# A transformer block on one core: where x + gate * bias is added, and when the MLP's rows are normed

## The chip, the cores and the metric

The kernel runs on one core of a Trainium2 chip. The metric is device time in microseconds (us) for one execution, as the median of several runs. One execution was also recorded by the hardware profiler. From that record come the profile (a page of summaries) and the trace behind it, which can be asked for waits, groups of instructions, stretches of time and a timeline. The engines are called by the profile's short names where a line is quoted: PE is TensorE's matmul, PEld its weight load, DVE is VectorE, ACT ScalarE, POOL GpSimd and SP SyncE, whose queue issues transfers.

## The reference

A conditioned transformer block (adaptive layer norm) in float32: batch B = 2, N = 2048 tokens, C = 576 features, 16 heads of 36, MLP width 2304.

```python
mod = silu(c) @ w_ada + b_ada
sh_msa, sc_msa, g_msa, sh_mlp, sc_mlp, g_mlp = split(mod, 6)
xn = _ln(x, 1e-6) * (1 + sc_msa) + sh_msa
q, k, v = heads(xn @ w_qkv + b_qkv)
q, k = _ln(q, 1e-5, qn_g, qn_b), _ln(k, 1e-5, kn_g, kn_b)
o = softmax(q @ k.T * 36**-0.5) @ v
x = x + g_msa * (o @ w_proj + b_proj)
xn2 = _ln(x, 1e-6) * (1 + sc_mlp) + sh_mlp
h = gelu(xn2 @ w1 + b1)
x = x + g_mlp * (h @ w2 + b2)
```

## The kernel before

The branch that runs is `block_of_small`. Its stages follow one another; each is a Python loop that is fully unrolled.

**Start.** `mod`, the shifts and scales of x, is computed from `w_ada`. Row tiles of 128 tokens are normed on VectorE (`rows_normed`: statistics L271, aggregate L273, root on ScalarE L275, reciprocal L277, scaling L278, and a copy on ScalarE L279), transposed by TensorE into PSUM (`transposed`, L348 and L349) and scaled by ScalarE on their way out (`modulated`, L356).

**For each of two batches: inputs, attention, outputs.** `inputs` makes q, k and v of 16 token tiles (matmuls L370 and L381). `attend` runs 8 pairs of heads (p) by 4 query blocks of 512 (qb) by 4 groups of keys (g): 128 steps a batch. A step computes scores (L981), their exponentials on ScalarE (L985) and the product with the values of the step before (L994); VectorE adds that product to the tile `ot` (copied by L1040 for g = 0, added by L1042 after). Eight PSUM banks go round: a step takes eight for scores and one for the sums. When a query block is finished (`finish`), its sums of exponentials go to DRAM and back, spread over partitions (`den`, L1009 and L1010 on SP's queue). The function `divided` comes steps later: a reciprocal (L1013), a product (L1014) and five transfers to `qo` on SP's queue (L1019). What comes later is kept in a list of lists, `later`: `later[3]` is run three steps on. `take_q` and `take_k` fetch the next block's queries (SP's queue) and the next pair's keys (GpSimd's queue, L764 and L767); the small operations that split their last rows (L777, L778) are put into `later` as well. `hooks` holds functions that are called at a step (p, qb, g).

`outputs` projects the 16 token tiles (L370 and L381 again). For tile t, `residual(t)` loads x by GpSimd's queue (L1071) into a scratch tile, `biased(t)` adds gate * bias on GpSimd (L1075), `evicted` multiplies the PSUM tile by the gate on VectorE (L1080), and `summed` adds the two on VectorE (L1087) and stores the row tile in `x1_dram` (L1088). In the first batch the scratch tiles are pieces of `kr`, which held the keys; in the second they are a pool of twelve. In the second batch `outputs` also runs, between its tiles, the first MLP block's loads, norms and transposes, and five sums of w1's parts on VectorE (`weight_sums`, L1244 to L1248), whose operands `wr` and `wb` SP's queue loads.

**First MLP product.** It is done by a scheme with seven products instead of eight (m = 1 to 7) over 8 blocks of 512 tokens; each block has 9 jobs, and two jobs make one pass of the loop. `whole_part` (L1320) multiplies m = 2, 4, 5, 6, 7, 3, 1; `halved_part` (L1334) adds the last 64 features; `gelu_stored` copies the m = 1 sum out of PSUM on ScalarE (L1346), combines the products on VectorE (L1347 to L1354) in the tile `cs`, applies gelu (L1358) and stores. Four sums of tokens in the tiles `ss` (`token_sums`, L1291 to L1294) are needed before m = 5, 6 and 3. `ahead(job)` prepares the next block: its `at(offset)` names the token tile whose base job lies `offset` jobs back. A tile is loaded one job ahead of its base job (L823, GpSimd's queue, three tiles in turn), normed in it, transposed in the job after it (L1379, then L1385 on ScalarE) and its last chunk in the second job after. Bases are jobs 0, 2, 4 and 6 of each block. Nine being odd, they fall on the first job of a pass in even blocks and on the second in odd ones. Five sums of w2's parts on VectorE (`later_sums`, L1397) stand at the ends of some passes.

**Second MLP product** (`second_product`, L1470), which the change leaves alone.

**Order.** TensorE's instructions are in program order throughout, VectorE's in inputs, in attention and from the second batch's outputs on. The other engines' orders come from a planner that works with estimated times. Waits are put in by the framework, from the regions that instructions read and write; a tile in a new pool waits for the users of the tiles that had its place.

Of the kernel before, what the change touches and what calls it, by code (L numbers as in the profile page):

```python
# [8 lines left out]
F32 = mybir.dt.float32  # L9
# [3 lines left out]
ALU = mybir.AluOpType  # L13
# [3 lines left out]
P = 128  # L17
# [14 lines left out]
def dit_block(  # L32
# [309 lines left out]

    def transposed(src, tail):

        ps = s_tile()
        t4, t1 = ps[:, 0, :], ps[:, 1, :]
        for k in range(FULL):
            nc.tensor.transpose(t4[:, k * P : (k + 1) * P], src[:, k * P : (k + 1) * P], ident)  # L348
        nc.tensor.transpose(t1[:, :P], tail, ident)  # L349
        return t4, t1  # L350

    def modulated(dst, src, which, b):

        t4, t1 = transposed(*src)
        for k in range(NKC):
            nc.scalar.activation(  # L356
                dst[:, k, :],
                t4[:, k * P : (k + 1) * P] if k < FULL else t1[:, :P],
                AF.Identity,
                bias=mod[:, which, k, b : b + 1],  # L360
                scale=mod[:, which + 1, k, b : b + 1],
            )
# [353 lines left out]
    def block_of_small():  # L716
# [114 lines left out]

        def input_by_feature(b, rows):
            xnt = xs["pool"].tile([P, NKC, P], F32, name="xnt", bufs=2)
            modulated(xnt, rows, 0, b)
            return xnt
# [127 lines left out]
        def attend(b, pool, hooks):  # L963
# [65 lines left out]
            for p, qb, g in [*steps, (None, None, None)]:  # L1029
# [5 lines left out]
                if behind is not None:  # L1035
                    bp, bqb, bg, bpts = behind
                    acc = values(bp, bpts)
                    if bg == 0:
                        ot = pool.tile([P, BLK], F32, name="ot", bufs=2)
                        nc.vector.tensor_copy(ot, acc)  # L1040
                    else:
                        nc.vector.tensor_tensor(ot, acc, ot, ALU.add)  # L1042
                    if bg == NG - 1:
                        later[3].append(finish(bp, bqb, ot))
                if (p, qb, g) in hooks:
# [8 lines left out]
        def output_weights(b):  # L1054
            pool, close = opened("wp", side="right")
            wp = pool.tile([P, FULL, C], F32, name="wp")
            wp4 = pool.tile([P, 1, HALF], F32, name="wp4")
            nc.sync.dma_start(out=wp, in_=w_proj[0:512, :].rearrange("(k p) f -> p k f", p=P))
            last_chunk(wp4, w_proj, 1, HALF)
            return (wp, wp4, gate_rows(pool, 0, b), gate_rows(pool, 1, b), pool), close  # L1060

        def outputs(b, weights, between, scratch):


            wp, wp4, g1, gb1, pool = weights
            x1s = {}

            def residual(t):
                if t < NT:
                    x1s[t] = scratch[t % len(scratch)]  # L1070
                    nc.gpsimd.dma_start(out=x1s[t], in_=x[b, t * P : (t + 1) * P, :])  # L1071

            def biased(t):
                if t < NT:
                    nc.gpsimd.tensor_tensor(x1s[t], x1s[t], gb1, ALU.add)  # L1075

# [6 lines left out]
            def summed():  # L1083
                while products:
# [4 lines left out]
                    residual(t + 6)  # L1089
                    biased(t + 3)  # L1090

# [5 lines left out]
            for t in range(6):  # L1097
                residual(t)
            for t in range(3):
                biased(t)  # L1100
            for t0 in range(0, NT, 4):
# [27 lines left out]
        close_psum = opened_psum(s=4)  # L1129
        xnt = input_by_feature(0, (x_first[:, :512], x_first[:, 512:]))  # L1130
        loaded = [tile_loaded(x[0, t * P : (t + 1) * P, :], nc.sync) for t in (1, 2)]
        weights, close_weights = input_weights()
        for b in range(B):
# [32 lines left out]
            def output_opened():  # L1166
# [7 lines left out]
                (4, 0, 1): output_opened,  # L1174
            }
            if b == 0:
                hooks |= {
                    (0, 2, 1): ada_opened,
                    (1, 0, 2): ada_gates,
                    (2, 0, 2): ada_feature_rows,  # L1180
                    (2, 0, 3): ada_features,
                }
            with tc.manual_schedule(engines={mybir.EngineType.DVE}):
                attend(b, att, hooks)
# [4 lines left out]
            if b + 1 < B:  # L1189
# [4 lines left out]
                }  # L1194
                outputs(b, wp, between, [kr[:, c, a * 640 : a * 640 + C] for c in range(4) for a in range(3)])
                xnt = opening["xnt"]
# [82 lines left out]
        hidden = [m2.tile([P, NF, PAIR], F32, name="hidden0")]  # L1279
        m1, close_m1 = opened("m1")  # L1280
        ss = {m: m1.tile([P, 2, PAIR], F32, name=f"s{m}") for m in (1, 2, 4)}
        stack = ExitStack()
# [20 lines left out]
        def whole_part(n, f, side, first):  # L1303
# [13 lines left out]
            out_m = sums_of(side)  # L1317
            for m in (2, 4, 5, 6, 7, 3, 1):
                for k in range(2):
# [22 lines left out]
        def gelu_stored(n, f, side):  # L1342
            cs = m1.tile([P, 5, PAIR], F32, name="cs", bufs=2)
            flat = ps_m[side].rearrange("p b c -> p (b c)")
# [16 lines left out]
        def ahead(job):  # L1361
# [7 lines left out]

            if todo := at(-1):  # L1370
                rows_ahead[todo] = mlp_loaded(*todo, nc.gpsimd)
            if todo := at(0):
                rows_ahead[todo] = tile_normed(rows_ahead[todo])
# [34 lines left out]
        rows_ahead = {}  # L1408
        rows_ahead[1, 0] = mlp_loaded(1, 0, nc.gpsimd)
        token_sums(0)  # L1410
# [131 lines left out]
```

## Time and profile before

| What | Value |
|---|---|
| Median of 3 runs (lowest to highest) | 3267.62 us (3267.26 to 3267.93) |
| Profiled execution, own time | 3270.42 us |
| Its span, first to last instruction | 3268.6 us |
| Busy: PE, PEld, DVE, ACT, POOL | 3218.1, 1888.4, 1456.7, 1504.6, 318.0 us |
| First batch: attention from, outputs from, next inputs' end | 269, 1051, 1384 us |
| Second batch: outputs from | 2137 us |
| First MLP product, second MLP product from | 2216, 2771 us |

In a line of the timeline the columns are start, duration, engine, source line, operation, tiles (out<-in), shapes and count; brackets hold the engine's idle time just before, and what ended it. A line of the waits names who waited, the line that released it, the total, the number of times and the longest. "L278" is line 278 of the kernel. The ends of matmul records are modelled and overlap the next start, so losses on TensorE are best counted from start to start.

### The profile page before, as it was taken

Reading aid. Unit: us, or ns where it says so; the run is one execution under the profiler, and the core shown is the slowest. Engines: PE = TensorE matmul, PEld = TensorE weight load, DVE = VectorE, ACT = ScalarE, POOL = GpSimd, SP = SyncE. Lnnn points to the kernel's source line nnn. Section 1 sums busy time; section 2 is a strip of 40 time slices with the busy share of each in tenths; the row PEclk is TensorE's granted clock in tenths of the full one; section 3 lists DMA queues with packets and bytes.
Section 4 is the critical chain, followed back from the end, with each engine's and each line's share of the span. In section 5 each row is a group of like instructions: output and inputs, shape, how many; then the busy total and the mean of one; then the engine's idle time right before and its main releaser. Section 6 shows DMA issues by size and latency. Waiting matters only on the chain.

```text
span 3268.6 us, 46758 instructions
## 1 busy us (share of the span) xinstructions
PE 3218.1 (98%) x18143; PEld 1888.4 (58%) x18143; DVE 1456.7 (45%) x2073; ACT 1504.6 (46%) x2952; POOL 318.0 (10%) x369
## 2 busy tenths in 40 slices
PE   7999999999999999999999999999999999999998
PEld 5775333333334777633333333367888888777776
DVE  4664333333333466533333333364455444454454
ACT  2335666666665033466666666614554552000000
POOL 1111001001100111100000000040000000111111
PEclk9999999999999999999999999999999999999999
DMA  3112312112211411121121211154322222433321
GB/s 129 26 27 64 86 44 69 47 43 56 55 36 30 144 29 24 27 64 36 44 47 42 45 43 35 35 184 150 118 83 81 88 78 97 168 120 119 116 102 38
DMA packets 122803, 234.28 MB, mean 72 GB/s; under 512 B 21891, under 2 KB 64844, under 8 KB 120524
## 3 DMA queue, kind: packets, MB, share of 16 engines
q1 hardware_dynamic: 104244, 182.07, 18.3%
q0 software_dynamic: 17600, 47.64, 5.5%
q8 instruction: 146, 2.39, 0.3%
q10 hardware_dynamic: 728, 1.48, 0.2%
q14 instruction: 85, 0.70, 0.1%
HBM read 125.96 MB, written 56.91 MB: 56 GB/s over the span
## 4 chain that ended last, share of the span: by engine, by line
PE 95%; DMA 1%; issue 1%; DVE 1%; ACT 0%; POOL 0%; SPq 0%; DVEq 0%; POOLq 0%; ACTq 0%
PE b L994 28%; PE b L981 19%; PE s L370 14%; PE s L1470 14%; PE m L1320 12%; PE m L1334 2%; PE s L381 2%; PE one L1320 2%; PE s L884 1%; PE t L1379 1%; DMA wb<-in_w_dram 1%; PE s L348 0%; DMA wq<-in_w_qkv_dram 0%; DVE xt L278 0%; DMA wa<-in_w_ada_dram 0%
## 5 line engine op out<-in xcount | busy, mean ns | idle before, releaser
L985 ACT ACTIVATE pt<-b 128x512 f32<-128x512 f32 x2048 | 1058.0, 610 | 487.2 <-PE b L994 271.1
L994 PE MATMUL b<-pt,vt 128*64 128x512 f32 x4096 | 935.1, 599 | 0.0
L994 PEld LDWEIGHTS b<-pt,vt 128*64 128x64 f32 x4096 | 271.8, 136 | 581.4 <-issue 439.4
L981 PE MATMUL b<-qm,km 32*128 32x512 f32 x4096 | 567.9, 614 | 2.0 <-DVE vt L936 1.6
L1042 DVE TENSOR_TENSOR ot<-b,ot 128x512 f32<-128x512 f32 x192 | 132.7, 691 | 656.2 <-PE b L994 656.2
L981 PE MATMUL b<-qe,ke 16*128 16x512 f32 x2048 | 423.5, 789 | 0.0
L370 PE MATMUL s<-wq,xnt 128*128 128x288 f32 x1536 | 393.3, 411 | 1.1 <-DMA wq<-in_w_qkv_dram 1.1
L1470 PE MATMUL s<-ws,as 128*128 128x288 f32 x1440 | 351.8, 406 | 0.0
L981 PEld LDWEIGHTS b<-qm,km 32*128 32x128 f32 x4096 | 192.4, 185 | 271.8 <-ACT pt L985 206.5
L370 PEld LDWEIGHTS s<-wq,xnt 128*128 128x128 f32 x1536 | 286.8, 191 | 92.9 <-issue 18.5
L1470 PEld LDWEIGHTS s<-ws,as 128*128 128x128 f32 x1440 | 273.7, 190 | 75.5
L1013 DVE RECIPROCAL den<-den 128x512 f32<-128x512 f32 x64 | 213.9, 3342 | 1.8 <-DMA den<-den_dram 1.8
L1320 PE MATMUL m<-s,wb 128*128 128x256 f32 x864 | 210.2, 379 | 4.5 <-DVE s L1294 3.5
L1320 PE MATMUL m<-xnt,wb 128*128 128x256 f32 x864 | 214.5, 384 | 0.0
L1040 DVE COPY ot<-b 128x512 f32<-128x512 f32 x64 | 44.2, 691 | 339.1 <-PE b L994 321.0
L1320 PEld LDWEIGHTS m<-s,wb 128*128 128x128 f32 x864 | 164.1, 190 | 27.5 <-DVE s L1294 3.9
L1320 PEld LDWEIGHTS m<-xnt,wb 128*128 128x128 f32 x864 | 159.6, 191 | 32.9 <-issue 12.6
L981 PEld LDWEIGHTS b<-qe,ke 16*128 16x128 f32 x2048 | 108.8, 184 | 114.1 <-issue 112.8
L1347 DVE TENSOR_TENSOR cs<-m,cs 128x512 f32<-128x512 f32 x72 | 49.7, 691 | 236.6 <-ACT cs L1346 158.6
L1358 ACT ACTIVATE cs<-cs,b_sb 128x512 f32<-128x512 f32 x144 | 103.9, 722 | 88.6 <-DVE cs L1353 88.6
L1470 PE MATMUL s<-ws,hidden 128*128 128x288 f32 x576 | 142.3, 406 | 0.0
L356 ACT ACTIVATE xnt<-s,mod 128x128 f32<-128x128 f32 x180 | 66.6, 458 | 159.8 <-PE s L349 159.8
(160 smaller groups left out, 2572.0 us busy)
## 6 DMA issues: line engine op xcount, KB each, us to landing
gelu<-cs SPq DMA_DIRECT2D x144, 256.0 KB
hidden<-gelu SPq DMA_DIRECT2D x16, 2304.0 KB
den<-den_dram SPq DMA_DIRECT2D x128, 128.0 KB
qm<-qo SPq DMA_DIRECT2D x192, 64.0 KB
xr<-x_dram SPq DMA_DIRECT2D x32, 288.0 KB
out_dram<-y POOLq DMA_DIRECT2D x32, 288.0 KB, 3.7
qe<-qo SPq DMA_DIRECT2D x256, 32.0 KB
qo<-ot SPq DMA_DIRECT2D x104, 72.0 KB
```

The lines of the kernel that those rows point to most:

```text
L356: nc.scalar.activation(dst[:, k, :], t4[:, k * P : (k + 1) * P] if k < FULL else t1[:, :P], AF.Identity, bias=mod[:, which, k, b : b + 1], ...
L370: nc.tensor.matmul(outs[a], stationary(k, a), moving(k, a), start=(first and k == 0), stop=(not first and k == FULL - 1),)
L381: nc.tensor.matmul(outs[a], stationary(FULL, a)[r], moving(FULL, a)[r], start=first, stop=not first)
L981: nc.tensor.matmul(ps, k[r, keys], q[r, :], start=first, stop=not first)
L985: nc.scalar.activation(pt[:, h, :], banks[2 * c + h], AF.Exp, scale=SCALE)
L994: nc.tensor.matmul(acc[64 * h : 64 * h + 64, :], vt[:, v0 : v0 + 64], pt[:, h, :], start=pt is pts[0][0], stop=pt is pts[-1][0],)
L1013: nc.vector.reciprocal(den, den)
L1042: nc.vector.tensor_tensor(ot, acc, ot, ALU.add)
L1320: nc.tensor.matmul(out_m[m], wb[:, slot[m], k, f * P : (f + 1) * P], moving[m](k), start=k == 0 and (m == 1 or (first and m in (2, 5, 6))) ...
L1334: nc.tensor.matmul(out_m[m], w[r, f * P : (f + 1) * P], a[r, FULL, t * PAIR : (t + 1) * PAIR], start=first and m != 4, stop=not first and ...
L1358: nc.scalar.activation(part, part, AF.Gelu, bias=b1_sb[:, g : g + 1])
L1470: nc.tensor.matmul(ms[m], stationary[m][:, f, :], ws[m][:, f, :], start=(f == 0), stop=(f == HF - 1))
```

## The change

- `residual_begun` runs in attention, at hooks (3 + t // 4, t % 4, 3) for t = 0 to 16: GpSimd's queue loads a row tile of x into `spare` (a piece of `kr`), the tile before it gets gate * bias added on GpSimd and is stored in `x1_dram`. For t = 0 it loads the gate row as well. `outputs` then loads from `x1_dram` in place of x, and adds no bias. In attention GpSimd's instructions are in program order.
- In the last pair of heads `divided` is put two steps on, not three.
- In the first MLP product a token tile is normed one job ahead of its base job and loaded three jobs ahead; tile (1, 0) is still normed in job 0, and two tiles are loaded before the loop.
- The `cs` tiles are two fixed ones, allocated ahead of the `ss` tiles. In the first job m = 1 comes third.
- The very first transposes write their last chunk into a second PSUM tile.

```diff
@@ -340,18 +340,18 @@
         nc.vector.tensor_copy(xn[:, C:], xn[:, 512:576])
         return xn[:, :512], xn[:, 512:]
 
-    def transposed(src, tail):
+    def transposed(src, tail, apart=False):
 
         ps = s_tile()
-        t4, t1 = ps[:, 0, :], ps[:, 1, :]
+        t4, t1 = ps[:, 0, :], (s_tile() if apart else ps)[:, 1, :]
         for k in range(FULL):
             nc.tensor.transpose(t4[:, k * P : (k + 1) * P], src[:, k * P : (k + 1) * P], ident)
         nc.tensor.transpose(t1[:, :P], tail, ident)
         return t4, t1
 
-    def modulated(dst, src, which, b):
-
-        t4, t1 = transposed(*src)
+    def modulated(dst, src, which, b, apart=False):
+
+        t4, t1 = transposed(*src, apart)
         for k in range(NKC):
             nc.scalar.activation(
                 dst[:, k, :],
@@ -829,9 +829,9 @@
         def input_rows(b, t, queue):
             return tile_normed(tile_loaded(x[b, t * P : (t + 1) * P, :], queue))
 
-        def input_by_feature(b, rows):
+        def input_by_feature(b, rows, apart=False):
             xnt = xs["pool"].tile([P, NKC, P], F32, name="xnt", bufs=2)
-            modulated(xnt, rows, 0, b)
+            modulated(xnt, rows, 0, b, apart)
             return xnt
 
         def inputs(b, weights, work, xnt, loaded):
@@ -1041,7 +1041,7 @@
                     else:
                         nc.vector.tensor_tensor(ot, acc, ot, ALU.add)
                     if bg == NG - 1:
-                        later[3].append(finish(bp, bqb, ot))
+                        later[2 if bp == NPAIR - 1 else 3].append(finish(bp, bqb, ot))
                 if (p, qb, g) in hooks:
                     later[1] = (hooks[p, qb, g]() or []) + later[1]
                 later.append([])
@@ -1057,22 +1057,32 @@
             wp4 = pool.tile([P, 1, HALF], F32, name="wp4")
             nc.sync.dma_start(out=wp, in_=w_proj[0:512, :].rearrange("(k p) f -> p k f", p=P))
             last_chunk(wp4, w_proj, 1, HALF)
-            return (wp, wp4, gate_rows(pool, 0, b), gate_rows(pool, 1, b), pool), close
+            return (wp, wp4, gate_rows(pool, 0, b), pool), close
+
+
+        spare = [kr[:, c, a * 640 : a * 640 + C] for c in range(4) for a in range(3)]
+
+        def residual_begun(b, t):
+
+            if t == 0:
+                nc.gpsimd.dma_start(out=spare[2], in_=gate_dram[1, b, :].partition_broadcast(P))
+            if t < NT:
+                nc.gpsimd.dma_start(out=spare[t % 2], in_=x[b, t * P : (t + 1) * P, :])
+            if t > 0:
+                rows = spare[(t - 1) % 2]
+                nc.gpsimd.tensor_tensor(rows, rows, spare[2], ALU.add)
+                nc.gpsimd.dma_start(out=x1_dram[b, (t - 1) * P : t * P, :], in_=rows)
 
         def outputs(b, weights, between, scratch):
 
 
-            wp, wp4, g1, gb1, pool = weights
+            wp, wp4, g1, pool = weights
             x1s = {}
 
             def residual(t):
                 if t < NT:
                     x1s[t] = scratch[t % len(scratch)]
-                    nc.gpsimd.dma_start(out=x1s[t], in_=x[b, t * P : (t + 1) * P, :])
-
-            def biased(t):
-                if t < NT:
-                    nc.gpsimd.tensor_tensor(x1s[t], x1s[t], gb1, ALU.add)
+                    nc.gpsimd.dma_start(out=x1s[t], in_=x1_dram[b, t * P : (t + 1) * P, :])
 
             def evicted(ts):
                 for t in ts:
@@ -1087,7 +1097,6 @@
                     nc.vector.tensor_tensor(x1, x1, product, ALU.add)
                     nc.gpsimd.dma_start(out=x1_dram[b, t * P : (t + 1) * P, :], in_=x1)
                     residual(t + 6)
-                    biased(t + 3)
 
             def placed(t):
                 for do in between.get(t, ()):
@@ -1096,8 +1105,6 @@
             products = []
             for t in range(6):
                 residual(t)
-            for t in range(3):
-                biased(t)
             for t0 in range(0, NT, 4):
                 tiles, sums = [], []
                 for t in range(t0, t0 + 4):
@@ -1127,7 +1134,8 @@
 
 
         close_psum = opened_psum(s=4)
-        xnt = input_by_feature(0, (x_first[:, :512], x_first[:, 512:]))
+
+        xnt = input_by_feature(0, (x_first[:, :512], x_first[:, 512:]), True)
         loaded = [tile_loaded(x[0, t * P : (t + 1) * P, :], nc.sync) for t in (1, 2)]
         weights, close_weights = input_weights()
         for b in range(B):
@@ -1173,6 +1181,9 @@
                 (0, 1, 1): last_inputs_done,
                 (4, 0, 1): output_opened,
             }
+            hooks |= {
+                (3 + t // NBLK, t % NBLK, 3): lambda t=t: residual_begun(b, t) for t in range(NT + 1)
+            }
             if b == 0:
                 hooks |= {
                     (0, 2, 1): ada_opened,
@@ -1180,7 +1191,7 @@
                     (2, 0, 2): ada_feature_rows,
                     (2, 0, 3): ada_features,
                 }
-            with tc.manual_schedule(engines={mybir.EngineType.DVE}):
+            with tc.manual_schedule(engines={mybir.EngineType.DVE, mybir.EngineType.Pool}):
                 attend(b, att, hooks)
             close_att()
             close_psum()
@@ -1192,7 +1203,7 @@
                     9: [lambda: opening.update(rows=input_rows(b + 1, 0, nc.scalar))],
                     14: [lambda: opening.update(xnt=input_by_feature(b + 1, opening["rows"]))],
                 }
-                outputs(b, wp, between, [kr[:, c, a * 640 : a * 640 + C] for c in range(4) for a in range(3)])
+                outputs(b, wp, between, spare)
                 xnt = opening["xnt"]
                 close_wp()
 
@@ -1278,6 +1289,8 @@
         ws = {m: m2.tile([P, HF, HALF], F32, name=f"ws{m}") for m in (2, 5, 3, 4, 1, 6, 7)}
         hidden = [m2.tile([P, NF, PAIR], F32, name="hidden0")]
         m1, close_m1 = opened("m1")
+
+        css = [m1.tile([P, 5, PAIR], F32, name=f"cs{i}") for i in range(2)]
         ss = {m: m1.tile([P, 2, PAIR], F32, name=f"s{m}") for m in (1, 2, 4)}
         stack = ExitStack()
         banks = stack.enter_context(tc.tile_pool(name="ps_m", bufs=1, space=PSUM, reuse_waits="tile"))
@@ -1315,7 +1328,8 @@
                 7: lambda k: a[:, k, t[1]],
             }
             out_m = sums_of(side)
-            for m in (2, 4, 5, 6, 7, 3, 1):
+
+            for m in (2, 4, 1, 5, 6, 7, 3) if n == f == 0 else (2, 4, 5, 6, 7, 3, 1):
                 for k in range(2):
                     nc.tensor.matmul(
                         out_m[m],
@@ -1340,7 +1354,7 @@
                 )
 
         def gelu_stored(n, f, side):
-            cs = m1.tile([P, 5, PAIR], F32, name="cs", bufs=2)
+            cs = css[side]
             flat = ps_m[side].rearrange("p b c -> p (b c)")
             two = lambda i: flat[:, i * PAIR : (i + 2) * PAIR].rearrange("p (a c) -> p a c", a=2)
             nc.scalar.copy(cs[:, 4, :], ps_m1[:, side, :])
@@ -1367,9 +1381,9 @@
                 m, g = divmod(job - offset, HF)
                 return (m + 1, g // 2) if m + 1 < NB and g % 2 == 0 and g // 2 < TPB else None
 
-            if todo := at(-1):
+            if todo := at(-3):
                 rows_ahead[todo] = mlp_loaded(*todo, nc.gpsimd)
-            if todo := at(0):
+            if todo := (1, 0) if job == 0 else at(-1):
                 rows_ahead[todo] = tile_normed(rows_ahead[todo])
             for offset, chunks in ((1, range(FULL)), (2, (FULL,))):
                 if todo := at(offset):
@@ -1406,7 +1420,8 @@
             nc.sync.dma_start(out=hidden[q % len(hidden)], in_=gelus[n][g])
 
         rows_ahead = {}
-        rows_ahead[1, 0] = mlp_loaded(1, 0, nc.gpsimd)
+        for i in range(2):
+            rows_ahead[1, i] = mlp_loaded(1, i, nc.gpsimd)
         token_sums(0)
         for job in range(0, NB * HF, 2):
             (n0, f0), (n1, f1) = divmod(job, HF), divmod(job + 1, HF)
```

## The prediction

> **What bounds the kernel now.** I read the page's busy times first. TensorE is the bound:
>
> ```profile
> PE 3218.1 (98%) x18143; PEld 1888.4 (58%) x18143; DVE 1456.7 (45%) x2073; ACT 1504.6 (46%) x2952; POOL 318.0 (10%) x369
> ```
>
> None of the edits takes a matmul away, so only TensorE's idle time can be won: 3268.6 less 3218.1 is 50.5 us, of which 8.9 lie after the last matmul. Next, TensorE's waits (waiter, released by: us in total, times, longest):
>
> ```profile
> PE t L1379 <- DVE xt L278: 7.9, 10, 3.0
> PE t L1379 <- DVE x_first L278: 4.0, 5, 3.0
> PE m L1320 <- DVE s L1294: 3.5, 1, 3.5
> PE s L348 <- DVE xt L278: 2.5, 1, 2.5
> PE s L348 <- DVE product L1080: 2.2, 1, 2.2
> PE s L370 <- DVE ot L1042: 1.9, 1, 1.9
> ...
> PE s L348 <- PE s L303: 0.6, 1, 0.6
> ```
>
> All of these are places that the diff touches: the MLP's token transposes (L1379), entry to the MLP (L1294; a further 1.1 us by L1291), the second batch's output stage (L348 twice), the first batch's (L370), the first transposes. Between 260 and 1051 us and between 1384 and 2186 us no matmul waits over 0.12 us: attention has nothing to win.
>
> The waits understate the loss. Third, TensorE's timeline (start, us), an undisturbed transpose and a late one:
>
> ```profile
> 2317.66 1.03 PE L1320 MATMUL one<-xnt,wb 128*128 128x256 f32 x4
> 2318.52 0.27 PE L1379 MATMUL t<-ident,x_first 128*128 128x128 f32 x1
> 2318.72 2.00 PE L1334 MATMUL m<-xnt,wr 64*128 64x256 f32 x16
> ...
> 2407.12 1.03 PE L1320 MATMUL one<-xnt,wb 128*128 128x256 f32 x4
> 2411.17 1.08 PE L1379 MATMUL t<-ident,x_first 128*128 128x128 f32 x4 [3.02 <-DVE x_first L278]
> 2412.18 3.07 PE L1334 MATMUL m<-xnt,wr 64*128 64x256 f32 x16
> ```
>
> A record's modelled end overlaps the next start. Counted from start to start, a transpose follows its group by 0.86 us undisturbed, here by 4.05: 3.19 lost, not 3.02. And the 16 matmuls behind it take 3.07 us for 2.00. The stretches (length, PE busy, PEld, DVE, ACT, POOL, clock, DMA) say why:
>
> ```profile
> 2407.57:2410.98 3.41, 0.58 (x3) 0.18 (x1) 1.91 (x6) 1.95 (x3) 0.00 (x0) 1.00 0.00 1
> 2410.98:2414.39 3.41, 3.22 (x14) 2.58 (x16) 0.12 (x2) 2.33 (x6) 0.00 (x0) 0.50 0.00 0
> ```
>
> The granted clock halves after the stall. Past the start, the record of the granted clock shows this at 2226.66 (3.4 us), 2410.98 (3.4), 2503.14 (6.8) and 2540.69 (3.4), each behind one of the four stalls of about 3 us or more, and behind no shorter one.
>
> **What the Trainium skill says.** "TensorE: Matmul & The Clock Gate", Part 1, says that the array drops to half rate after an idle window of some 3.4 us. The trace agrees in size and goes further: a window with 0.58 us of work, even one with 1.31 (from 2223.25), is followed by clock 0.50. "SBUF — State Buffer", "SBUF: two separate sides", says that GpSimd and a VectorE operation with two SBUF inputs, or in a two-port mode, lock each other out for whole instructions. The trace agrees. VectorE and GpSimd in the second output stage:
>
> ```profile
> 2186.66 6.16 DVE L1246 TENSOR_TENSOR wb<-wb 128x2304 f32<-128x2304 f32 x1
> ...
> 2197.58 2.55 DVE L1247 TENSOR_TENSOR wb<-wb 128x2304 f32<-128x2304 f32 x1
> ...
> 2186.27 4.13 POOL L1075 TENSOR_TENSOR x<-x,gate 128x576 f32<-128x576 f32 x3
> ```
>
> The same sum takes 6.16 us beside three adds and 2.55 alone. L1080, with one input in PSUM, takes 756 ns alone and 758 in seven overlaps.
>
> **The parts.** (a) *MLP normalization a job sooner.* Fifteen of the transposes wait for L278, all in even blocks: there the norm is queued at the start of a job and its transpose comes one job later, while VectorE first finishes the job before. Three are 3 us late because a weight sum (L1397, 2.85 us) stands ahead. Moved one job forward, the norm, with its root and copy on ScalarE, comes some 7.5 us sooner in the order, so it occupies the same idle piece of VectorE one job pair before its use. In the odd blocks this order exists already, and they show no stall. Loads also move two jobs sooner; GpSimd's queue already runs ahead until a tile is free and lands in 3.1 us. Gain: twelve short stalls, 0.41 each from start to start, 4.9; three long ones with their slow clock, by comparing equal transposes: 2401.83 to 2421.33 is 19.50 against 14.76 (2312.04 to 2326.80), 2530.59 to 2550.21 is 19.62 against 14.76, 2486.42 to 2515.40 is 28.98 against 22.97 (2630.49 to 2653.89 less its short stall). That is 4.7 + 4.9 + 6.0 = 15.6. Together **20.5**. Behind the moved norm VectorE queues gelu_stored; it had 3.3 us idle before that at 2414, so nothing new is late.
>
> (b) *Entry.* L1294 waits for a store:
>
> ```profile
> 2224.60 0.69 DVE L1294 TENSOR_TENSOR s<-xnt,s 128x512 f32<-128x512 f32 x1 [4.31 <-DMA x_dram<-x]
> ```
>
> The s tiles lie where the scratch tiles of t = 12 to 14 were (2304 bytes each, s tiles 2048). With two cs tiles of 5120 bytes ahead of them they lie on t = 4 to 7, stored long before. The cs tiles inherit the late stores, which land 8.4 us after the first MLP matmul; VectorE wants cs at about 9. From the first matmul to the tail transposes (2216.07 to 2237.42) it takes 21.35 us, undisturbed 14.65: 6.7 lost. With product m=1 third, the ss[1] sum (ready at +2.9) meets TensorE at +2.6, 0.3 lost; the others are in time. The norm of tile (1,0), not moved, ends at about +7.0 against +6.4: 0.7 lost. Gain 6.7 - 1.0 = **5.7**.
>
> (c) *Adds out of the output stage.* The waits at 2186 and 2197 cost 2.2 and 2.5, start to start 5.1. With no add, L278 (1.98 us there, 0.58 alone), L1245 (3.62) and L1246 (6.16, each 2.55 alone) give VectorE back 6.1 us. Then the transfer of wb is next late (L1245 waits 2.67 for it); it starts some 4 us sooner by (d). I leave 0.5: gain **4.6** (bounds 3 and 5.1). The residual's loads remain, from x1_dram in place of x.
>
> (d) *The last pair's division a step sooner.* At 1051 us the first output matmul waits for the last eviction, behind L1013 and L1014:
>
> ```profile
> 1046.29 3.34 DVE L1013 RECIPROCAL den<-den 128x512 f32<-128x512 f32 x1
> 1049.66 0.69 DVE L1014 TENSOR_TENSOR ot<-ot,den 128x512 f32<-128x512 f32 x1
> 1050.27 0.68 DVE L1042 TENSOR_TENSOR ot<-b,ot 128x512 f32<-128x512 f32 x1
> ```
>
> They leave a step (5.98 us) sooner; den is there (issued 1031.9, needed 1040.4). The eviction's 0.7 stays: gain **1.3**. In SP's order the five qo stores (3.87 us) leave sooner, thus the last den transfers and, behind those, wr and wb. In blocks 0 and 1 of that pair the division now shares its step with L777 and L778 (0.48 + 0.75): 0.69 + 1.23 + 3.34 + 0.69 = 5.95 of 5.98, just in time.
>
> (e) *First transposes.* The scale of x could start 0.3 sooner, but the first product waits for wq, landing at 24.1. **0**; bounds from -1.7 (a half-speed window less) to +0.5.
>
> (f) *What attention takes on.* Per batch 16 adds (1.41 us each, 22.6), 33 transfers (0.55 of GpSimd each, 18) and 9.4 MB more traffic (16 stores and 16 loads of 288 KB); SP loses one gate load. In program order these stand between the key transfers of take_k (L764, L767), which wait for the scores of the pair before (907.5 us of GpSimd idling in eleven waits). So four residual tiles run in a burst at a pair's start, behind keys needed 96 us later; of what is ahead of each take_k nothing waits for TensorE. VectorE's evictions (L1042, L1040) have an input in PSUM, as L1080; locked out are L1014, L778 and perhaps L777. A step with a division leaves VectorE idle 1.30 us, and the sums' bank is wanted 0.4 us after the eviction: one full lock-out of 1.41 fits. Three adds in the first batch's pair 6 (863.8 to 868.0) already show no stall. Cost 0; the trace cannot show all 32: bounds 0 and 32 x 1.41 = 45.
>
> **Sum**: 20.5 + 5.7 + 4.6 + 1.3 = 32.1 from 3270.4 (span 3268.6 and 1.8 around it): 3238.3. The median of the runs shown is 2.8 below that; part of this may be half-speed windows that fall otherwise when unprofiled, so I take half of it off: **3237**.
>
> **Rivals.** *Only the MLP wins:* wb still lands late and the entry waits for another tile: 3270.4 - 20.5 - 1.4 = 3248. For it: VectorE in the output stage waits for transfers as well as adds. *The norm gains nothing*, because ScalarE's root is put behind later work: 11.6 won, 3257. Against it: the odd blocks. *Slower: the lock.* If each add in attention delays an eviction by its own length, 45 are lost against 32 won: 3281. It decides from 1.0 us a tile. Against it: PSUM evictions untouched in the trace, and 1.30 + 0.4 us of room.
>
> **Chances.** Forecast 0.72, one of the two smaller wins 0.17, all lost again to within 0.2% (6.5 us, about what a measurement of this kernel can tell from no change) 0.03, slower 0.08. Range 3231 (every listed stall gone: 20.5 + 6.7 + 5.1 + 2.1 + 0.6 + 1.7 = 36.7) to 3251, which takes in the first rival.
>
> **What would show it.** Right: no wait at L1379 but the first, clock 1.00 from 28 us to the end, no L1294 wait for a store, L1246 at 2.55 us, GpSimd adds in bursts of four in pairs 3 to 6. Wrong: matmuls of attention (L981, L994) among TensorE's waits, or L1379 waiting for L278 again.

## The result, and the profile after

The changed kernel takes **3250.05 us** (median of 5 runs, 3247.01 to 3252.43) against 3267.62 (3265.43 to 3269.23): ratio **0.9946 [0.9931, 0.9960]**, 17.6 us less. The direction and the range held. The forecast was 13 us better than the result, and that is no single miss: three of its steps came out nearly to size, three were wrong, and the start was 2 us shorter, most of that by the landing of a transfer.

The page's busy times and TensorE's waits of the kernel after:

```profile
PE 3212.6 (99%) x18143; PEld 1884.8 (58%) x18143; DVE 1450.2 (45%) x2073; ACT 1496.4 (46%) x2950; POOL 354.1 (11%) x435
```

```profile
PE s L192 <- DMA wa<-in_w_ada_dram: 11.6, 3, 10.6
PE t L1393 <- DVE xt L278: 2.7, 1, 2.7
PE b L981 <- DVE ot L1040: 2.5, 2, 1.4
PE s L370 <- DMA wq<-in_w_qkv_dram: 1.6, 1, 1.6
PE s L303 <- DMA gb_rows<-rows_dram: 0.8, 1, 0.8
PE s L370 <- DVE ot L1042: 0.8, 1, 0.8
```

Four of the waits shown before are gone: that of the MLP's transposes (L1379, now L1393) fifteen times over, the entry's (L1294, now L1304, 0.2 us left), and the second output stage's two on L348. The wait for the last eviction of attention has fallen from 1.9 to 0.8. But one transpose waits 2.7 us, and attention, where nothing had waited past its first matmul, now has **two waits on L981 for VectorE's tile ot**. GpSimd is busy 36 us longer (x435 for x369), which by itself costs nothing.

By stage, from the first matmul of each to the first of the next, in the profiled executions:

| us | before | after |
|---|---|---|
| start and first inputs (to the first matmul of attention) | 269.5 | 265.9 |
| attention, first batch | 781.6 | 784.5 |
| outputs, first batch | 72.0 | 72.0 |
| inputs, second batch | 241.3 | 241.3 |
| attention, second batch | 773.1 | 776.6 |
| outputs, second batch | 78.6 | 73.6 |
| first MLP product | 554.6 | 532.0 |
| second MLP product | 489.0 | 489.0 |
| after the last matmul | 8.9 | 14.2 |
| span | 3268.6 | 3249.3 |

So the MLP and the second output stage gave about what they should, some of it was lost again in both attentions, and 5.4 us more lie behind the last matmul. The first output stage, out of which 16 adds were taken too, did not move at all.

### The profile page after: what moved, and what is told of

Its sections match the earlier page's. It is cut to its first block, busy times and chain, and to the rows that moved or that the text cites. A ratio compares the mean times of both kernels' runs of the same rounds, so it can differ in the third digit from the quotient of the medians.

```text
span 3249.3 us, 46887 instructions
## 1 busy us (share of the span) xinstructions
PE 3212.6 (99%) x18143; PEld 1884.8 (58%) x18143; DVE 1450.2 (45%) x2073; ACT 1496.4 (46%) x2950; POOL 354.1 (11%) x435
## 4 chain that ended last, share of the span: by engine, by line
PE 95%; issue 2%; DMA 1%; DVE 1%; POOL 0%; SPq 0%; ACT 0%; DVEq 0%; POOLq 0%; ACTq 0%
PE b L994 28%; PE b L981 19%; PE s L370 14%; PE s L1485 14%; PE m L1334 12%; PE m L1348 2%; PE s L381 2%; PE one L1334 2%; PE s L884 1%; PE t L1393 0%; PE s L348 0%; DMA wq<-in_w_qkv_dram 0%; DMA qo<-ot 0%; DMA wa<-in_w_ada_dram 0%; PE b L192 0%
## 5 line engine op out<-in xcount | busy, mean ns | idle before, releaser
L994 PE MATMUL b<-pt,vt 128*64 128x512 f32 x4096 | 936.7, 599 | 0.0
L994 PEld LDWEIGHTS b<-pt,vt 128*64 128x64 f32 x4096 | 272.1, 137 | 582.8 <-issue 441.3
L981 PE MATMUL b<-qm,km 32*128 32x512 f32 x4096 | 570.7, 614 | 3.3 <-DVE ot L1040 2.5
L981 PE MATMUL b<-qe,ke 16*128 16x512 f32 x2048 | 424.3, 788 | 0.0
L1042 DVE TENSOR_TENSOR ot<-b,ot 128x512 f32<-128x512 f32 x192 | 132.8, 692 | 650.3 <-PE b L994 649.8
L981 PEld LDWEIGHTS b<-qm,km 32*128 32x128 f32 x4096 | 192.8, 185 | 275.5 <-ACT pt L985 206.9
L1040 DVE COPY ot<-b 128x512 f32<-128x512 f32 x64 | 44.3, 692 | 343.7 <-PE b L994 315.7
L981 PEld LDWEIGHTS b<-qe,ke 16*128 16x128 f32 x2048 | 108.7, 184 | 114.7 <-issue 113.0
L1471 DVE TENSOR_TENSOR as<-hidden 128x1152 f32<-128x1152 f32 x80 | 139.0, 1801 | 0.0
```

What stands on the lines that cost most here:

```text
L981: nc.tensor.matmul(ps, k[r, keys], q[r, :], start=first, stop=not first)
L994: nc.tensor.matmul(acc[64 * h : 64 * h + 64, :], vt[:, v0 : v0 + 64], pt[:, h, :], start=pt is pts[0][0], stop=pt is pts[-1][0],)
L1471: nc.vector.tensor_tensor(stationary[m], x_, y_, op)
```

## The experiments

Four questions: does (a) alone give its 20.5; what took attention's time; what took the entry's; what the tail is. For attention there were two theories: the *transfers* put in front of VectorE's tile ot, or the *lock*, in which GpSimd's adds hold up VectorE's instructions. All edits are to the kernel after unless said. The runs of one kernel spread over up to 12.5 us, so an edit is judged here by the stretch of the profile that it touches, more than by the median.

**(a) alone, on the kernel before**

```diff
-            if todo := at(-1):
+            if todo := at(-3):
                 rows_ahead[todo] = mlp_loaded(*todo, nc.gpsimd)
-            if todo := at(0):
+            if todo := (1, 0) if job == 0 else at(-1):
                 rows_ahead[todo] = tile_normed(rows_ahead[todo])
```

(Two tiles are loaded before the loop, as in the change.)

> The kernel before, with the MLP token tiles normed a job sooner and loaded two jobs sooner, and nothing else of the change. By the prediction's own step (a): no L1379-type wait for L278 after the first tile, no half-speed window past 2231 us, first MLP product 20.5 us shorter than before (554.6): 534. Time 3267.6 - 20.5 = 3247 if the tail does not move. Rival: part of the 20.5 needs the other edits; then waits on L278 remain.

Measured: 3249.91, ratio 0.9946 [0.9930, 0.9963]; the first MLP product took 533.3 us for 554.6, so **(a) is worth 21.3** between these two profiles. Two further profiles with the MLP of before, shown below, have 551.9 and 553.0 there; against them it is 18.6 and 19.7. Most of the other waits of before stay in this kernel, as TensorE's waits show:

```profile
PE m L1320 <- DVE s L1294: 3.2, 1, 3.2
PE s L348 <- DVE product L1080: 2.5, 1, 2.5
PE s L370 <- DVE ot L1042: 1.9, 1, 1.9
```

This one edit has the ratio of the whole change. Everything else in it together came to nothing.

**Attention: adds without their transfers, transfers without their adds**

```diff
 without transfers:
-    nc.gpsimd.dma_start(out=spare[t % 2], in_=x[b, t * P : (t + 1) * P, :])
+    nc.gpsimd.memset(spare[t % 2], 0.0)
-    nc.gpsimd.dma_start(out=x1_dram[b, (t - 1) * P : t * P, :], in_=rows)
 (the residual is then loaded from x)
 without adds:
-    nc.gpsimd.tensor_tensor(rows, rows, spare[2], ALU.add)
```

> The changed kernel with the 32 adds kept, on tiles that GpSimd fills with zeros, and without the 32 loads and 32 stores in attention; the output stages load x itself, so gate * bias of the projection is left out of the result. Theory T: no wait of L1040 for qo<-ot above 6.4 us and no matmul stall over 0.5 us in attention; second batch's stretch 773 us. Rival L: stalls of 1 us and more stay, 776 us. The tail after the last matmul: if GpSimd's closing DRAIN (6.5 us changed, 1.1 us before) grows with the number of GpSimd transfers (320 against 254), it falls towards 1 us here (256 transfers).

> The changed kernel without the 32 GpSimd adds in attention, all transfers kept; it leaves out gate * bias of the projection. Measured so far: in attention the changed kernel loses about 1.7 us near 578 us and 3.4 us near 1669 us, both where the copy L1040 waits for qo<-ot transfers. Theory T (the burst of row-tile transfers at a pair's start delays the stores of ot, so its buffer comes free late): both losses stay, attention's two stretches at about 784 and 776.6 us. Rival L (the adds lock VectorE out): both go, 781 and 773 us, and L1040 no longer idles 8 us before it.

Measured, without transfers: one run, 3238.26; attention 782.1 and 773.0, no wait in it over 0.3 us. VectorE's timeline in this kernel shows the lock at work and costing nothing:

```profile
568.15 1.93 DVE L1014 TENSOR_TENSOR ot<-ot,den 128x512 f32<-128x512 f32 x1
570.15 0.69 DVE L1042 TENSOR_TENSOR ot<-b,ot 128x512 f32<-128x512 f32 x1
...
577.70 0.69 DVE L1040 COPY ot<-b 128x512 f32<-128x512 f32 x1 [6.86 <-DMA qo<-ot]
```

L1014 has two SBUF inputs and takes 1.93 us beside an add (0.69 before); L1042 and L1040, with one input in PSUM, take their 0.69. The 1.24 us fit into VectorE's idle time, as the prediction's room of 1.30 said. In the kernel after, three of VectorE's operations were held up beside adds (L777 at 585 took 2.03 us, L1014 at 762 took 2.05, L778 at 874 took 2.29), and no matmul waits at these places. The lock as the rival that costs time in attention is refuted.

Without adds, with the transfers: one run, 3247.78; attention 783.3 and 774.1, its stalls on L981 down to 0.5 us in all, though from start to start it still lost 1.4 us at 772 and 0.6 at 1669. Here the expectation was missed: the transfers alone should have kept both losses. So the transfers are necessary, but when their burst meets VectorE's copy depends on the adds between them as well; how, these runs don't settle.

What the transfers hold up is in VectorE's waits, for before and then after (total, times, longest):

```profile
DVE ot L1040 <- DMA qo<-ot: 11.7, 2, 6.0
```

```profile
DVE ot L1040 <- DMA qo<-ot: 28.0, 4, 8.0
```

L1040 opens a query block's sum in one of two ot tiles. It needs the tile that the division (L1014) finished and that SP's queue has still to store (qo). VectorE's timeline, then TensorE's, then SP's queue, in the kernel after:

```profile
578.87 0.69 DVE L1040 COPY ot<-b 128x512 f32<-128x512 f32 x1 [8.03 <-DMA qo<-ot]
```

```profile
579.62 0.69 PE L981 MATMUL b<-qm,km 32*128 32x512 f32 x1 [1.38 <-DVE ot L1040]
```

```profile
565.12 6.28 SPq L767 DMA_DIRECT2D qe<-qo  x3
571.45 1.83 SPq L764 DMA_DIRECT2D qm<-qo  x2
573.38 0.67 SPq L767 DMA_DIRECT2D qe<-qo  x1
574.15 1.56 SPq L1019 DMA_DIRECT2D qo<-ot  x2
```

L1014 was done at 568.85, but the qo stores were issued only at 574.15, 5.3 us later; they ended at about 578.8. It is not the landing that became slower: from the end of their issue to L1040 there are 3.2 us here and 3.1 at 1669, and 3.7 and 4.1 at the two waits of before (771 and 1668), where the stores were issued 2.4 and 1.6 us after the division. Ahead of them on SP's queue stand the loads of the next queries, whose issue is slow at a pair's start (6.28 us for the first three L767 here, 0.67 for the fourth). In the kernel without transfers L1014 was done 1.2 us later, the stores were issued at 573.12, 1.0 sooner, and L1040 began 1.2 us sooner.

The transfers are not the whole of it. From the end of the division to the issue of the stores it takes, at 579 and 1669, 2.3 and 1.6 us in the kernel before, 4.5 and 3.5 in a kernel with all the rest of the change and no move (last section below), and 5.3 and 5.2 in the kernel after. So more than half of the delay came with another part of the change. GpSimd's program order in attention is one that could do it, as it changes the order of take_k's transfers; no run tries that alone. The rest comes with the move, and in the kernel with no move no matmul of these attentions waits over 0.3 us. How transfers of one queue slow the issue on another isn't shown.

One such stall of 1.14 us, at 1670, was followed by a slow clock; the stretches of after (length, PE, PEld, DVE, ACT, POOL, clock, DMA share, GB/s):

```profile
1667.98:1671.39 3.41, 2.27 (x14) 0.64 (x10) 0.69 (x1) 1.08 (x2) 1.27 (x3) 1.00 0.47 175
1671.39:1674.80 3.41, 3.41 (x10) 0.97 (x10) 0.00 (x0) 1.09 (x2) 1.28 (x2) 0.50 0.58 191
```

With it, 3.44 us were lost there: the whole 3.5 of the second batch.

**Attention: take away what L1040 waits for, or move the loads**

```diff
 a third ot tile in the second batch:
-    ot = pool.tile([P, BLK], F32, name="ot", bufs=2)
+    ot = pool.tile([P, BLK], F32, name="ot", bufs=2 if b == 0 else 3)
 x loads on SP's queue:
-    nc.gpsimd.dma_start(out=spare[t % 2], in_=x[b, t * P : (t + 1) * P, :])
+    nc.sync.dma_start(out=spare[t % 2], in_=x[b, t * P : (t + 1) * P, :])
```

> The changed kernel with three ot tiles in the second batch, two as before in the first (no room for three there). Theory T: the loss near 1669 us (1.1 us of stall, then a half-speed window, 3.4 us in all) goes, the second stretch of attention falls from 776.6 to 773.2 us, the first batch's loss near 578 us stays; time 3.4 us less than the changed kernel, about 3246.6. Rival L: no difference in either batch.

> The changed kernel with the loads of x in attention on SP's queue in place of GpSimd's. SP's queue advances with the steps, so row tiles should come one by one over pairs 3 to 6 and not four in a burst at a pair's start. Theory T: L1040 waits no more for qo<-ot, no stall over 0.5 us in attention, 4 to 5 us less than the changed kernel in attention, about 3245 in all. Rival L: the same number of adds, the same losses, at other places. Risk for T: SP's queue holds a load back behind a wait, or takes queries late; then new stalls appear at L777. GpSimd's transfers fall to 288: if the closing DRAIN grows with them it is between 1.1 and 6.5 us.

Measured, third tile: 3247.46, ratio 0.9936 [0.9915, 0.9956]. The second batch's attention is back at 772.4, and VectorE's timeline shows the copy there waiting only for TensorE:

```profile
1665.80 0.69 DVE L1040 COPY ot<-b 128x512 f32<-128x512 f32 x1 [5.29 <-PE b L994]
```

The first batch, left with two tiles, kept its stall (1.32 us). That shows the path: transfers, SP's queue, qo store, ot, L981.

Measured, loads on SP's queue: 3243.73, ratio 0.9922 [0.9905, 0.9939]. The second batch has no stall (773.7); the first lost its stall at 580 but got one of 1.09 at 770 with a slow clock behind it (785.2). Moving the transfers to the other queue moves the stall, it doesn't remove it.

**Entry: which scratch tiles lie under the cs tiles**

```diff
-    outputs(B - 1, wp, between, [scratch.tile(...) for i in range(12)])
+    outputs(B - 1, wp, between, [scratch.tile(...) for i in range(12)][::-1])
```

> The changed kernel with the twelve scratch tiles of the second output stage used in reverse order of address, so that the last stored rows (t = 12 to 15) lie beyond the cs and ss tiles. Theory: the 2.7 us stall of the first MLP transposes (2223 us) comes from ScalarE's copy L1360 into cs, which waits for the late store and has the root of the norm queued behind it. Then the copy starts some 4 us sooner, the stall falls below 0.8 us, the half-speed window behind it goes (1.7 us), and the first MLP product takes 528 us in place of 532: about 3246. Rival: the norm is late by VectorE's own order (product, sums of tokens before it): the stall stays at 2.7 us.

Measured: the first MLP product took **528.0** for 532.0, as expected; the median, 3246.46, ratio 0.9931 [0.9914, 0.9947], is as expected too, but its four runs lie between 3241.46 and 3252.92, and the profiled one, the slowest, has attentions 2.1 and 1.5 us longer. ScalarE's timeline in the kernel after shows what was in the way:

```profile
2221.94 0.37 ACT L1360 COPY cs<-one 128x256 f32<-128x256 f32 x1 [13.61 <-issue]
2222.21 0.30 ACT L275 ACTIVATE std<-mv,eps 128x1 f32<-128x1 f32 x1
```

The copy into cs needs a scratch tile whose last store landed at 2221.64. The root of the first norm, L275, stands behind that copy on ScalarE, and the wait goes on, on VectorE and then on TensorE:

```profile
2222.54 0.16 DVE L277 RECIPROCAL rstd<-std 128x1 f32<-128x1 f32 x1 [2.71 <-ACT std L275]
2222.74 0.58 DVE L278 TENSOR_SCALAR xt<-xt,mv,rstd 128x576 f32<-128x576 f32 x1
```

```profile
2223.37 0.66 PE L1393 MATMUL t<-ident,xt 128*128 128x128 f32 x4 [2.67 <-DVE xt L278]
```

With the scratch tiles in reverse order the same copy waits for its product alone, and the transpose 0.4 us (ScalarE's timeline and TensorE's waits of that kernel):

```profile
2222.43 0.37 ACT L1360 COPY cs<-one 128x256 f32<-128x256 f32 x1 [8.50 <-PE one L1334]
```

```profile
PE t L1393 <- DVE xt L278: 0.4, 1, 0.4
```

**The tail: the last stores, and the number of GpSimd's transfers**

```diff
 last stores, on the kernel after and on the kernel before:
-    nc.gpsimd.dma_start(out=out[b, ...], in_=rows)
+    nc.scalar.dma_start(out=out[b, ...], in_=rows)
 64 more transfers, on the kernel before, as attention of the first batch begins:
+    for k in range(64):
+        nc.gpsimd.dma_start(out=extra, in_=x[...])   # 128 rows of 8 floats
```

> The changed kernel with the 32 output stores of the second MLP product issued from ScalarE's queue in place of GpSimd's. Theory D: GpSimd's closing DRAIN is long because of GpSimd's own transfers shortly before the end; with none, it falls from 6.5 to about 1 us and the tail after the last matmul from 14.2 to 9 us or less: about 3245. Rival: the DRAIN's length hangs on something else and varies from run to run; the tail stays near 14 us or moves without system.

> The kernel before with 64 further small loads (128 x 8 floats) on GpSimd's queue in the first batch's attention, results unused. The closing DRAIN of GpSimd so far: 1.124 us with 254 transfers, 1.287 with 256, 3.902 with 288, 6.514 with 320, a straight line of 81.7 ns a transfer. If it counts transfers whatever their size and place, it takes 6.35 us here with 318 and the tail grows from 8.9 to about 14. Rival: it hangs on bytes or on what is issued late; then it stays at 1.1.

> The kernel before with the 32 output stores of the second MLP product on ScalarE's queue: 222 GpSimd transfers. The straight line of 81.7 ns a transfer would be at nothing near 240, so the DRAIN is expected at 1.1 us or below and the tail no longer than the 8.9 us of before; if the line starts anew (a count that wraps), it is long again.

A kernel ends on GpSimd with an instruction called DRAIN, seen in the trace's records of GpSimd's sequencer. Before and after, it starts 6.9 us after the last matmul, and its length is the whole difference of the tails. With the number of transfers on GpSimd's queue beside it, over all the profiles (the last two kernels of the table come further down):

| Kernels | transfers | DRAIN, us | after the last matmul, us |
|---|---|---|---|
| before; (a) alone | 254 | 1.124 | 8.9; 9.2 |
| without transfers | 256 | 1.287 | 9.0 |
| x loads on SP's queue | 288 | 3.902 | 11.9 |
| 64 more | 318 | 6.351 | 14.4 |
| after; without adds; third ot tile; scratch reversed; without (d) | 320 | 6.514 or 6.515 | 14.2 to 14.5 |
| after, last stores on ScalarE's queue | 288 | 3.902 | 8.2 |
| before, last stores on ScalarE's queue | 222 | 8.393 | 9.1 |
| move in the second batch alone | 255 | 1.206 | 8.3 |
| no move | 222 | 8.392 | 8.2 |

From 254 to 320 these lie on a line of 82 ns a transfer: (6.514 - 1.124) / 66. The 64 small loads met their 6.35, so it goes by transfers and not by bytes. It could also go by their rows: all transfers that were added or taken away have 128. The 222 transfers did not give a still shorter DRAIN but 8.4 us, so the line does not go on below 254; why is open. With the last stores on another queue the DRAIN starts over 18 us before the last matmul ends and is hidden, even at 8.4. The kernel after with that edit: 3241.94, ratio 0.9919 [0.9903, 0.9936], with a tail 6.0 us shorter; before with it, one run: 3267.56, as before, since its DRAIN was short.

The 64 loads took more than the DRAIN: one run, 3309.49, attention 815.6. TensorE's waits in it:

```profile
PE b L981 <- DVE ot L1044: 25.1, 3, 23.0
```

The copy into ot (here L1044) stood 29.6 us for a qo store that was issued only at 351.63, though its division was done at 323.4. The waits of SP's queue show what held it:

```profile
SPq L244 <- POOL rows L240: 31.9, 1, 31.9
```

Ahead of the store on SP's queue stood a load (L244) into a tile that GpSimd first clears (L240, at 341.97), and on GpSimd that stood among the small loads, which all go into one tile and landed one after another, some 2.2 us each. So the end of the path is that of the kernel after, a store that comes late in SP's queue; what holds the queue is another thing.

**Without (d)**

```diff
-    later[2 if bp == NPAIR - 1 else 3].append(finish(bp, bqb, ot))
+    later[3].append(finish(bp, bqb, ot))
```

> The changed kernel with the last pair's division back at three steps. By step (d): first output matmul of the first batch waits 1.9 us again (0.8 changed), and in the second batch wr and wb start some 4 us later, so that one wait for L278 or a product of about 1 us comes back in the output stage: 1 to 2.5 us slower than the changed kernel, 3251 to 3252.5. Rival: SP's earlier order is worth nothing, only the 1.1 us at 1050.

Measured: 3256.24, ratio 0.9961 [0.9947, 0.9975]: 6.2 us more than after, where at most 2.5 were expected. The wait at 1054 is 1.95 us again, and a slow window behind it makes the first output stage 73.7; L348 waits 1.0 for L278 in the second (74.8), where wb comes later; and the first attention, 788.6, had a slow window of 6.8 us at 580 by the stall that after has too. The last may be the run's own; the first three are 1.1, 1.7 and 1.2 us, 4.0 in all.

**The move in the second batch alone, and none**

```diff
+    if begun(b):                # b == B - 1; False in the kernel without the move
         hooks |= {(3 + t // NBLK, t % NBLK, 3): lambda t=t: residual_begun(b, t) ...}
```

Both have three ot tiles in the second batch, the scratch tiles reversed and the last stores on ScalarE's queue; without the move, x is loaded and added in the output stage.

> The changed kernel with the addition in attention for the second batch alone (the first batch adds in its output stage as before, where the output stage took 72.0 us both ways), three ot tiles in the second batch, the scratch tiles reversed and the last output stores on ScalarE's queue. If the four causes found add up: attention 781.6 and 772.5 us, output stages 72.0 and 74, first MLP product 528, tail about 8.5 (255 GpSimd transfers, DRAIN about 1.2 us): about 3234, 16 less than the changed kernel. Rival: half-speed windows come back elsewhere and take 3 to 5 us of it.

> The kernel of the run beside it without any addition in attention: both output stages load x and add on GpSimd as before. What the move itself is worth in the second batch: the two stalls of the second output stage, 78.6 us before against 73.6 changed, come back in part (the division stays a step sooner): 77 us or more, total 3 to 5 us slower than with the move in the second batch. Rival: with wb loaded sooner the adds cost nothing, and the move is worth 0.

Measured: in the second batch alone **3234.78** (3234.03 to 3235.61), ratio **0.9899 [0.9884, 0.9914]**, within 1 us of the sum that its expectation made of the causes found; no move 3240.57 (3238.06 to 3240.95), ratio 0.9914 [0.9900, 0.9927]. The first is faster than the kernel before and the kernel after. The 5.8 us between them, a little more than expected, come from the second output stage: 73.6 for 80.6, less 1.7 in the attentions. VectorE without the move shows the lock, and then TensorE's wait, which has a slow window of 6.8 us behind it:

```profile
2169.63 4.28 DVE L1268 TENSOR_TENSOR wb<-wb 128x2304 f32<-128x2304 f32 x1
2175.44 3.40 DVE L278 TENSOR_SCALAR xt<-xt,mv,rstd 128x576 f32<-128x576 f32 x1
```

```profile
PE s L348 <- DVE product L1098: 4.0, 1, 4.0
```

The same weight sum in the kernel after, which has no adds there, takes 2.55 us. The first batch's output stage took 72.0 us with the move and without it: there is nothing to win in it. Its attention took 784.5 with the move, 783.1 and 782.0 in these two kernels without it.

## Why the prediction was right or wrong, step by step

The sum was 32.1; between the two profiles there are 19.3. That the range held, by 1 us, owes something to luck: its upper end had been set for the rival that only the MLP wins, and what filled it were most of one gain that did not come, (b), and two costs put at nothing, (f) and the tail. The sign that the prediction itself had named for being wrong, L981 among TensorE's waits, did appear, and the clock was not at 1.00 throughout: it was at 0.50 for 3.4 us from 1671 and from 2224.

| Step | predicted | measured | from |
|---|---|---|---|
| (a) norm a job sooner | 20.5 | 21.3 | that edit alone |
| (b) entry | 5.7 | 1.3 | first MLP product's 22.6 less (a) |
| (c) adds out of the output stage | 4.6 | 5.0 | 78.6 less 73.6 |
| (d) division sooner | 1.3 | 1.1 | wait at 1050: 1.95, now 0.82 |
| (e) first transposes, start | 0 | 2.1 | fifth product with the values (L994) at 303.9, now 301.8 |
| (f) attention from there on | 0 | -6.1 | 784.5 - (781.6 - 1.1) - 1.4 and 776.6 - 773.1 |
| tail | 0 | -5.4 | 8.9 to 14.2 |

**Right:** (a), (c) and (d), each within 1 us between these two profiles. Over the others (a) is 18.6 or more, and the second output stage takes 78.6 to 81.0 without the move and 73.6 to 74.8 with it. What held was pricing a stall from start to start against an equal undisturbed stretch, slow window included. In (c), VectorE's 6.16 us for L1246 became 2.55 for L1257; all of the gain is in the second batch.

**Wrong, (b):** the step that failed is "The cs tiles inherit the late stores, which land 8.4 us after the first MLP matmul; VectorE wants cs at about 9". That named the right tile and looked at the wrong engine. ScalarE's copy L1360 is the first to write cs, and the roots of the norms stand behind it; the root of tile (1,0) was wanted much sooner than cs. The wait removed from L1294 came back at L1393. The tile order reversed gave 4.0 of the 4.4 missing, and the same 528.0 in all three kernels that have it. The 1.3 that is left of (b) is within the spread: the kernels with the MLP of after take 530.3 to 533.4 there, that with (a) alone 533.3.

**Wrong, (f):** "of what is ahead of each take_k nothing waits for TensorE". True for the instructions of GpSimd's queue, but the prediction followed only that queue. Its transfers and SP's are under way together, and L1040's wait for qo stood in the trace of before already, 6.0 us long. The bounds of 0 to 45 were set for the lock, which costs nothing here. From start to start against the kernel before, the 6.1 are 3.44 by the stall and slow window at 1670, 1.7 by the stall at 580, and 0.5 and 0.4 at 771 and 867, where L1040 waits for qo as well. A good part of the stores' delay came with the rest of the change, as shown above, but costs nothing by itself: the kernel with no move has 782.0 and 772.4. Not all of the first batch's 2.6 need be the move's: the kernel that moves only the second batch's adds lost 1.2 there.

**Wrong, the tail:** taken as unchanged, though 66 transfers were added to the queue whose DRAIN closes the kernel. Nothing in one profile showed that its length goes with their number.

**The start, (e):** the prediction says that between 260 and 1051 us no matmul waits over 0.12 us. It passed over one, at 269.46. TensorE's waits, before and then after:

```profile
PE b L981 <- DVE vt L936: 1.6, 1, 1.6
```

```profile
PE b L981 <- DVE vt L936: 0.3, 1, 0.3
```

All kernels with two PSUM tiles in the first transposes have the 0.3 and start attention at 264.4 to 267.4, all without at 267.7 to 270.0. The rotation of the four PSUM tiles is shifted by one, which fits, but no run tries that by itself, and each of these kernels loses 1.3 to 1.5 us again in attention's first steps. Of the 2.1 that the kernel after keeps, 1.3 were there before the edit could act, by the landing of w_ada (TensorE waited 11.6 us for it, 13.3 before). From the first matmul behind w_ada's (L230) to the fifth product with the values, ten kernels with the edit took 281.6 to 284.8 us and four without it 284.2 to 285.0. So a gain of the edit's own isn't shown.

**The rivals.** *Only the MLP wins*, 3248, is nearest to the result, but not for its reasons: wb was not late and (c) came. *The norm gains nothing* is refuted by (a) alone, and for (b)'s one tile its mechanism, a root behind other work on ScalarE, is just what happened. *The lock* is refuted as a cost in attention and shown as one in the second output stage.

## What to carry to other kernels

When work is moved into a stage that seems to have room, ask first which waits there end with a transfer, on whichever queue, and what the moved transfers will do to those; VectorE's wait for qo was on record before the change, long though harmless. When a buffer is laid over another's place, follow the new tile's first writer and all that stands behind that on its engine. Price a stall with the slow window that may follow it, and keep the last stores off GpSimd's queue when much has gone over that queue.

## What the runs showed of the hardware

GpSimd's closing DRAIN grows by 82 ns with each transfer of 128 rows on its queue from 254 (1.124 us) to 320 (6.514), and is 8.39 us at 222.

A stretch of 3.41 us (a window) need not be nearly idle to be followed by one at half the granted clock. "TensorE: Matmul & The Clock Gate", Part 1, of the Trainium skill speaks of an idle window. In attention, a window with PE busy for 2.27 of 3.41 us was followed by clock 0.50 (from 1667.98, above), and in five further such windows, of four other kernels, PE was busy for 2.03 to 2.44; in the kernel before, outside attention, windows with 1.62 and 2.22 (from 2182.29 and 2195.94) were not. Nearly all matmuls of the first use 16 or 32 rows of the array (L981); whether that is the reason wasn't tried. Which stalls are followed by such a window differs between nearly equal kernels: those of 1.38 and 1.32 us at 580 in the kernel after and in that with three ot tiles were not, one of 0.97 at 1668 (last stores on ScalarE's queue) was. Part of the spread from 3247.0 to 3252.4 may be this.
